# Last attention layer of a four-layer graph network on one Trainium2 core: probabilities with nodes on partitions, squares copied directly, and residual, input and result transfers issued from POOL

## Chip, core and metric

The kernel runs on one core of one Trainium2 chip. The time is the device time of one execution in microseconds (us), the median of three runs. In what follows PE is TensorE, DVE VectorE, ACT ScalarE, POOL GpSimd and SP SyncE; PEld is PE's loading of weights.

## What is computed

32 graphs of 512 nodes with 256 channels pass through four layers, all in float32 with one shared adjacency matrix `adj` of 512 x 512. Every layer has the form `x = x + L(relu(layernorm(x)))`. L0 is a two-step network with an unmasked and a masked graph attention, L1 a masked graph attention with one head, L2 an eight-head transformer block. The change touches L3, a graph attention with four heads of 64 channels:

```
q = (h @ W).reshape(B, N, 4, 64)
e = e_src[:, :, None, :] + e_dst[:, None, :, :]     # e_src, e_dst: q against the two halves of a
e = where(e >= 0, e, 0.2 * e)
e = where(adj > 0, e, -9e15)
out = elu(einsum('bijh,bjhd->bihd', softmax(e, axis=2), q))
```

So for each head a 512 x 512 matrix of probabilities is made from two vectors, and multiplied with 512 x 64 values. A node without neighbours gets the mean of all values.

## The kernel before

**Order.** The program is built as a list of operations of all 32 graphs, each with its engine, an estimated length, and what it reads and writes (`Graph.op`). `Plan.order` then places them like a list scheduler, at most six graphs in flight (`IN_FLIGHT`): of the operations that can start earliest the one with the earliest due time goes first. The due time comes from the graph's number times `PERIOD`, less the work behind the operation, plus a table of shifts by position (`SHIFTS`). Each engine then executes its instructions in this fixed order and waits for the others by semaphores. Buffers are taken in the same pass: `cell` (a part of 128 x 4 KB, 32 of them; a `Quad` is four in a row), `row`, `bank` (PSUM, 8), and in DRAM `page` and `sheet`.

**Transfers.** All are issued from SP (`transfer`): x is read twice per graph (`load`, L960), residuals are put away in DRAM pages and fetched again (`put_away` L967, `fetched` L973), the result is stored (L1588). L0 and L2 turn their layer input round by 32 x 32 squares: DVE transposes the squares (L636), then `crossed` writes them to a page (L615) and reads them back with the squares in place (L622). The eight heads of L2 do the same with their probabilities through a sheet (L1386 on DVE, L1391, L1399).

**Layer 3.** The input is transposed by PE (L655) and copied from PSUM by ACT (L663). The projection (L704) gives values and, for each head, three terms. `gat_probabilities` makes the probabilities already transposed, with the summed-over node on partitions. For each head PE spreads three vectors over all partitions by 4 transposes each (`rows_ps`, L720): the far term, a bias row, and the near term. DVE finds each row's masked maximum (L791, its output thrown away); POOL works the bias out of it (L806 to L809); ACT copies its row (L730); POOL adds the row to the transposed mask in two instructions (L821); DVE takes the maximum of two branches, which stands for the leaky relu, and adds it (L832, 4 per head); ACT takes the exponential (L840, 4 per head). POOL adds the probabilities up (L1484, L1488), a PE matmul with ones sums them (L1523), 16 matmuls give the output (L1502), and PE turns output and sums round (L1539). DVE scales by the reciprocal (L1548, L1551, L1561). Isolated nodes come apart from this: POOL and PE form the mean (`lonely`, L851, L852, L859), POOL spreads it (L870) and adds it (L1572).

Of the kernel before, what the change touches and what calls it, by code (L numbers as in the profile page):

```python
# [13 lines left out]
ALU = mybir.AluOpType  # L14
# [25 lines left out]
FLOOR = -(2.0**60)  # L40
TINY = 1e-30
# [3 lines left out]
CELL = NC * (C + 5)  # L45
ROW = N + 10
SMALL = 320
BUFFERS = {"cell": 32, "row": 7, "page": 48, "sheet": 12}
# [6 lines left out]
PERIOD = 50.7  # L55
# [3 lines left out]
    72, 50, 37, 26, 40, 30, 9, 57, 9, 9, 9, 9, 50, 27, -10, -39, 3, -6, 21, -19, -30, -122,  # L59
    -182, -23, -9, -33, 39, 5, -2, 1, -49, 1, 1, 0, -66, 1, 1, 1, 1, -16, 1, -38, -1, -71, -1,  # L60
    0, -23, 1, 2, -22, 1, 3, 1, -103, 1, 5, 1, -19, 1, 1, 19, 1, -26, 1, -3, 1, 1, 1, 14, 5, 0,
    1, 1, -10, 1, -2, 0, 0, 0, 1, 0, -1, 0, -1, 6, 0, -115, 19, 0, 7, -25, -6, 0, -32, -35, 0,
    68, 0, 35, 0, 93, -3, 2, 24, -51, 18, -11, 0, -7, 1, -75, 1, 1, 55, 0, 26, -26, 4, 3, 0,
    -39, -1, -162, -3, -56, -2, -13, 1, -20, -2, -37, -87, -26, -9, -7, -1, -27, -9, -52, -40,
    6, -52, -18, 0, -6, -4, 2, -5, -23, -88, 0, -14, -42, 12, -11, -1, -2, 6, -7, -10, -1, -49,
    -29, -3, -1, -23, 2, 0, -84, 10, -16, -46, -3, 7, 7, -17, 0, 0, 0, 0, -18, 0, 4, 144, 2, 0,
    -3, 0, -7, 2, -24, 27, -28, 31, -92, 47, -25, -10, 1, 0, -3, 0, 109, 0, -1, -75, -1, 0, 0,
    -3, 0, -7, -45, 0, 41, -1, 2, -7, 69, -15, -49, -3, -3, 0, 22, -97, -17, 4, -12, -9, 4, -53,
    -11, -1, -1, -5, 17, 5, 72, 47, 46, 74, 146, -16, -51, 41, -3, -13, -15, 2, 0, 1, 49, -18,
    -5, 30, 3, 4, 0, 0, -1, 0, 18, 14, -12, -32, 78, -1, 37, -82, -4, 7, -6, 0, 9, -3, -12, 9,  # L70
    0, -70, 20, 0, -10, 0, -1, 0, 23, 0, 0, -33, -10, 28, 83, 95, 37, 17, 76, -5, -36, -119,
    -25, -1, 92, 3, 0, 2, -3, 0, -24, 1, 0, -10, -5, -3, -36, -2, -46, -24, -68, 25, -10, -11,
    -13, -5, -2, -29, -22, -1, -1, -13, -2, 3, 14, 0, 0, 0, 28, 7, -83, -101, 7, 46, -9, -54,
    -46, 44, -24, 99, -5, -1, 0, 0, 75, 0, 0, 0, -10, 0, 1, 6, 0, 14, 0, 23, 13, -17, 53, 6, 87,
    -7, -16, 7, 3, 5, -1, -71, -87, 15, -12, 0, 11, 0, 0, 0, 8, 0, 0, -9, -8, 0, 23, 0, 0, -80,
    2, 0, 18, 0, 0, -3, 0, 0, 105, -13, -36, -11, -81, -30, -85, -143, -51, -24, -71, -29, -116,
    -48, -84, -82, -187, -154, -123, -175, -94, -43, -87, -62, 6, -91, -111, -160, -332, -388,
    -421, -351, -608, -395, -425, -396, -421, -341, -408, -335, -348, -464, -413, -372, -375,
    -378, -330, -297, -285, -312, -291, -315, -190, -199, -193, -90, -130, -236, -99, 76, -225,
    -189, -251, -299, -395, -387, -220, -242, -187, -183, -124, -28, -137, -109, -189, -108,  # L80
    -163, -117, -33, -55, -60, -125, -183, -244, -216, -176, -221, -264, -255, -199, -296, -271,
    -259, -434, -424, -521, -444, -340, -233, -214, -298, -180, -115, -52, -68, -145, -240,
    -205, -240, -241, -326, -236, -241, -474, -309, -46, -175, -128, -162, -177, -202, -326,
    -320, -212, -315, -229, -218, -238, -255, -252, -253, -294, -281, -196, -99, -190, 0, -59,
    -31, 0, -31, 3, -6, 2, 0, 2, -13, 0, 0, 0, 0, 16, 0, 141, -61, 0, 0, 0, -77, -2, -15, -29,
    -84, -35, -22, -60, -26, -26, -15, -26, -229, -39, -46, -103, -103, -16, -128, -41, -4, -61,
    -7, 35, -2, -9, 23, 3, 2, -22, -73, 5, -12, 2, 2, 2, -6, 2, 2, -5, 3, 2, 64, -18, 3, -11, 3,
    -24, 2, 2, 2, 3, 3, 42, 3, 1, 3, -26, 1, 3, -80, 17, -29, 27, -4, 3, 3, 3, 3, 3, 3, 3, -42,
    3, 0, -10, -36, -8, -69, -213, 23, -10, -20, 25, 26, 33, -18, 68, -12, -53, 17, 91, 94, 5,
    111, 25, 57, 164,  # L90
# [318 lines left out]
def adj_preln_kernel(  # L409
# [73 lines left out]
    self_biasT = const.tile([P, NC, N], BF, name="self_biasT")  # L483
    alone = const.tile([P, NC], FP, name="alone")
# [11 lines left out]
    l3_sb = weights(W_3, "l3_sb", TERMS * GAT_HEADS)  # L496
# [27 lines left out]
    ]  # L524
    smalls = [work.tile([P, SMALL], FP, name=f"smalls{k}") for k in range(IN_FLIGHT)]
# [15 lines left out]
    out_v = out.rearrange("b (c p) f -> b p c f", p=P)  # L541

    class Graph:
# [29 lines left out]
        def transfer(self, reads, writes, kbytes, emit, load=False):  # L573
            self.op("sp", 0.45, reads, writes, emit)
            self.op("dma", kbytes / RATE, reads, writes, lambda: None, 2.2 if load else 1.0)
# [200 lines left out]
        def gat_probabilities(self, holder, term, n, bias, biasT, own=False, after=()):  # L776
# [51 lines left out]
            for j in range(NC):  # L828
# [13 lines left out]
                    ),  # L842
                )
            return p, top

        def lonely(self, v, n):

            add = Buffer("row", 2, n)
# [116 lines left out]
        def put_away(self, src):  # L965
            page = Buffer("page", *src.shape)
            self.transfer([src], [page], 512, lambda: nc.sync.dma_start(page.ap, src.ap))  # L967
            return page
# [679 lines left out]
```

## Time and profile before

| | |
|---|---|
| median of 3 runs | 4420.88 us (4417.97 to 4422.98) |
| the profiled execution | 4422.42 us, span of its instructions 4420.6 us |
| mean granted PE clock | 0.979 |
| moved by DMA | 867.22 MB, 196 GB/s |
| busy: PE, DVE, POOL, ACT | 4170.8, 3662.7, 3034.1, 2924.3 us |

The span runs from the first instruction to the last. Busy time is the time in which an engine has at least one instruction, and a matmul's end is modelled, so that PE can be busy without being at its peak. The page cuts the span in 40 slices and gives busy tenths; it follows the chain of work that ended last; it lists groups of instructions by line with their count, busy time, mean duration and the idle time before them; and it lists DMA issues with their median time to landing. The trace answers the same questions for any stretch. Fp32 matmuls on full operands show as two instructions each.

### The profile page before, as it was taken

To read this page: it belongs to the slowest core of one execution; us is meant where nothing else is said; L and a number is where in the kernel's file an instruction comes from. 1 tells how busy PE (TensorE), PEld (TensorE's weight loads), DVE (VectorE), ACT (ScalarE), POOL (GpSimd) and SP (SyncE) were. 2 spreads that over 40 slices of the span, in tenths; PEclk is the share of its full clock that TensorE was granted. 3 is DMA by queue.
4 is the path that set the end of the run, shared out by engine and by line. 5 is a ranking of instruction groups with operands and counts; after the bars stand their busy time and mean duration, and the time that the engine had idled before them with its cause. 6 is when DMAs were issued, how large, how long until landed. Compare 5 with 4: busy or idle time off the path is not lost. (4 is left out here: it accounts for less than half of the span.)

```text
span 4420.6 us, 69315 instructions
## 1 busy us (share of the span) xinstructions
PE 4170.8 (94%) x21648; PEld 2583.3 (58%) x21648; DVE 3662.7 (83%) x9016; ACT 2924.3 (66%) x6309; POOL 3034.1 (69%) x3119
## 2 busy tenths in 40 slices
PE   6999999999999999999999999999999999999765
PEld 3656556665566666566666556666656666655332
DVE  3577888888888888888888888888889888888873
ACT  2556666777676667667667767666766766676653
POOL 1424766777776677776677777667777766777677
PEclk9999999999999999999999999999999999999877
DMA  3287667766767766766777667677667677766760
GB/s 121 84 226 218 187 190 220 218 202 181 215 199 211 224 200 201 204 204 194 222 215 204 201 200 211 194 224 210 205 205 206 192 217 219 201 200 186 231 175 29
DMA packets 441504, 867.22 MB, mean 196 GB/s; under 512 B 35248, under 2 KB 119728, under 8 KB 441136
## 3 DMA queue, kind: packets, MB, share of 16 engines
q1 hardware_dynamic: 439520, 862.78, 66.4%
q8 instruction: 173, 2.83, 0.3%
q14 instruction: 195, 1.60, 0.1%
q10 hardware_dynamic: 1616, 0.01, 0.0%
HBM read 443.23 MB, written 419.43 MB: 195 GB/s over the span
## 5 line engine op out<-in xcount | busy, mean ns | idle before, releaser
L1386 DVE STREAM_TRANSPOSE cells<-cells 128x512 f32<-128x512 f32 x1024 | 702.4, 698 | 148.8 <-ACT cells L1378 148.5
L1378 ACT ACTIVATE cells<-cells,smalls 128x512 f32<-128x512 f32 x1024 | 736.1, 719 | 114.0 <-DVE smalls L1367 105.8
L1367 DVE CUSTOM_DVE_ANT_0 cells<-bank,mask_bias 128x512 f32<-128x512 f32 x1024 | 686.9, 674 | 21.6 <-PE bank L1347 20.6
L821 POOL TENSOR_TENSOR cells<-mask_biasT,row 128x1024 f32<-128x1024 bf16 x320 | 682.3, 2155 | 16.2 <-ACT row L730 16.2
L791 DVE CUSTOM_DVE_ANT_0 masked<-bank,mask_bias 128x512 f32<-128x512 f32 x768 | 520.5, 678 | 71.1 <-PE bank L720 64.7
L683 PE MATMUL bank<-cells,mlp_sb 128*128 128x512 f32 x1024 | 473.1, 600 | 19.8 <-DMA cells<-page 13.2
L704 PE MATMUL bank<-fc_sb,cells 128*128 128x256 f32 (+1 forms) x2048 | 474.7, 381 | 1.5 <-DVE smalls L1367 0.8
L927 PE MATMUL bank<-cells 128*128 128x260 f32 x2048 | 465.1, 383 | 1.1 <-ACT cells L840 0.9
L603 ACT ACTIVATE cells<-cells,smalls 128x256 f32<-128x256 f32 x768 | 408.1, 592 | 74.7 <-POOL smalls L596 49.7
L1159 PE MATMUL bank<-cells 128*128 128x512 f32 x1024 | 450.9, 597 | 0.0
L927 PEld LDWEIGHTS bank<-cells 128*128 128x128 f32 x2048 | 387.9, 190 | 87.1 <-issue 24.9
L840 ACT ACTIVATE cells<-cells,smalls 128x512 f32<-128x512 f32 x512 | 348.5, 726 | 114.7 <-DVE cells L832 114.6
L704 PEld LDWEIGHTS bank<-fc_sb,cells 128*128 128x128 f32 x2048 | 376.9, 189 | 76.5 <-DVE cells L1442 19.0
L586 DVE BATCH_NORM_STATS2 smalls<-cells 128x6 f32<-128x256 f32 x768 | 311.3, 405 | 110.4 <-POOL cells L1222 101.3
L883 ACT ACTIVATE cells<-cells 128x512 f32<-128x512 f32 (+1 forms) x256 | 188.1, 735 | 292.9 <-DVE cells L946 111.3
L832 DVE SCALAR_TENSOR_TENSOR cells<-bank,smalls,cells 128x512 f32<-128x512 f32 x512 | 354.1, 740 | 30.5 <-POOL cells L821 27.0
L720 PEld LDWEIGHTS bank<-ident,smalls 128*128 128x128 f32 x2176 | 254.3, 141 | 212.6 <-issue 84.2
L720 PE MATMUL bank<-ident,smalls 128*128 128x128 f32 x2176 | 325.9, 284 | 54.2 <-POOL smalls L809 30.0
L1159 PEld LDWEIGHTS bank<-cells 128*128 128x128 f32 x1024 | 194.1, 193 | 230.2 <-issue 228.7
L1484 POOL TENSOR_TENSOR cells<-cells 128x1024 f32<-128x1024 f32 x128 | 302.3, 2372 | 19.2 <-PE bank L1502 8.4
L683 PEld LDWEIGHTS bank<-cells,mlp_sb 128*128 128x128 f32 x1024 | 186.0, 191 | 218.5 <-issue 170.3
L1347 PE MATMUL bank<-cells 32*128 32x512 f32 x2048 | 305.8, 644 | 5.7 <-DVE smalls L1367 4.8
(141 smaller groups left out, 8503.9 us busy)
## 6 DMA issues: line engine op xcount, KB each, us to landing
sheet<-cells SPq DMA_DIRECT2D x256, 1024.0 KB, 5.3
cells<-sheet SPq DMA_DIRECT2D x1024, 256.0 KB, 5.4
page<-cells SPq DMA_DIRECT2D x256, 512.0 KB, 3.4
cells<-page SPq DMA_DIRECT2D x192, 512.0 KB, 6.1
cells<-in_x_dram SPq DMA_DIRECT2D x64, 512.0 KB, 7.3
cells<-page SPq DMA_DIRECT2D x256, 128.0 KB, 2.9
out_dram<-cells SPq DMA_DIRECT2D x32, 512.0 KB, 5.4
mlp_sb<-in_L_gnn_mlp_w_dram SPq DMA_DIRECT2D x2, 512.0 KB, 6.7
```

The source lines that it names most:

```text
L603: lambda c=c: act.activation(xn[:, c, :], src[:, c, :], func, bias=off[:, c : c + 1], scale=rstd[:, c : c + 1],),
L683: lambda k=k, s=s, i=i, m=m, mm=mm: pe.matmul(mm.ap, w[:, k, cols + m * P : cols + (m + 1) * P], s.rows(i), start=(k == 0), stop=(k == nk ...
L704: pe.matmul(mm[:, :n], src[k // 2].nodes(k % 2, c), w[:, k, cols : cols + n], start=(k == 0), stop=(k == nk - 1),)
L720: pe.transpose(bc[:, c * P : (c + 1) * P], col(c).to_broadcast([P, P]), ident)
L791: lambda c=c: dve.tensor_tensor_reduce(masked, f2_ps.ap, bias[:, c, :], 1.0 - ALPHA, FLOOR, op0=ALU.add, op1=ALU.max, accum_out=top[:, c : ...
L821: lambda half=half: pool.tensor_add(p[half].ap, biasT[:, 2 * half : 2 * half + 2, :], w_row[:, None, :].to_broadcast([P, 2, N]),),
L832: lambda j=j, ph=ph, i=i: dve.scalar_tensor_tensor(ph[:, i, :], f1_ps.ap, term(2)[:, j : j + 1], ph[:, i, :], op0=ALU.max, op1=ALU.add,),
L927: pe.matmul(mm[:, :w1], p[j // 2][:, j % 2, c * P : (c + 1) * P], v[:, j, :], start=(j == 0), stop=(j == NC - 1),)
L1159: pe.matmul(mm.ap, h1[jh][:, i, m * P : (m + 1) * P], p[jh][:, i, :], start=(jh + i == 0), stop=(jh + i == 2),)
L1367: dve.tensor_tensor_reduce(tile(), sc[h].ap.rearrange("p (j f) -> p j f", j=NC), mask_bias[:, c, :].rearrange("p (j f) -> p j f", j=NC), - ...
L1378: lambda h=h, c=c, tile=tile: act.activation(tile(), tile(), AF.Exp, scale=-1.0, bias=low[:, c, h : h + 1], accum_out=sums[:, c, h : h + 1],),
L1386: dve.transpose(squared, squared)
```

## The change

Layer 3's probabilities are made with their own node on partitions. The input is turned round by `turned_round` instead of by PE. Per head one vector is spread by 4 PE transposes (`square_row`, its columns in the order of the squares), DVE adds mask and row and keeps both the sum and its maximum, POOL and ACT make the bias from the maximum, ACT applies Prelu with the near term as bias, then the exponential with its row sum accumulated, and DVE transposes the 32 x 32 squares. The squares of two heads are then copied from SBUF to SBUF by 16 transfers of 128 KB issued from SP (`squares_crossed`), each from 32 partitions to 32 partitions, and PE multiplies with the transposed result. The separate sums, the third term and the path for isolated nodes fall away in this layer (a row of equal masked values has equal probabilities). The nodes are then in square order, so the last residual is fetched in four quarters and the result stored in four quarters, and a mask in square order is made once at the start.

The pages' stores and loads, the second read of x and the first read of later graphs, the four quarters and the result are issued from POOL (`aside`); the transfers of `crossed`, the sheets, the direct squares and the loads at the start stay on SP. One `cell` more and three `row` fewer are held; `PERIOD` and all of `SHIFTS` are new. The diff, without `SHIFTS` and with small edits cut:

```diff
--- before
+++ after
-CELL = NC * (C + 5)
-ROW = N + 10
-SMALL = 320
-BUFFERS = {"cell": 32, "row": 7, "page": 48, "sheet": 12}
+CELL = NC * (C + 4)
+ROW = N + 8
+SMALL = 336
+BUFFERS = {"cell": 33, "row": 4, "page": 48, "sheet": 12}
...
-PERIOD = 50.7
+PERIOD = 53.2
...
-    self.op("dma", kbytes / RATE, reads, writes, lambda: None, 2.2 if load else 1.0)
+def transfer(self, reads, writes, kbytes, emit, load=False, issue=0.45, lag=2.2):
+    self.op("sp", issue, reads, writes, emit)
+    self.op("dma", kbytes / RATE, reads, writes, lambda: None, lag if load else 1.0)
+def aside(self, reads, writes, kbytes, emit, load=False):
+    self.op("pool", 1.2, reads, writes, emit)
+    self.op("dma", kbytes / RATE, reads, writes, lambda: None, 2.8 if load else 1.6)
...
+def square_row(self, holder, col, dst):
+    bc = Buffer("bank", N)
+    def emit():
+        for c in range(NC):
+            pe.transpose(
+                bc.ap.rearrange("p (q c i) -> p q c i", q=NC, i=SQUARE)[:, :, c, :],
+                col(c).to_broadcast([P, P]),
+                ident,
+            )
+    self.op("pe", 0.47, holder, [bc, *dst], emit)
+    return bc
+def masked_probabilities(self, holder, far, near, n, table, p, tile, parts, sums=None):
+    bias, key = table
+    f2_ps = self.square_row(holder, far, [p])
+    top = self.small(f"top{n}", NC)
+    m = self.small(f"m{n}", NC)
+    for c in range(NC):
+        self.op(
+            "dve", 0.77, [f2_ps, [(key, c, q) for q in range(P // SQUARE)]], [top, parts(c)],
+            lambda c=c: dve.tensor_tensor_reduce(
+                tile(c),
+                f2_ps.ap.rearrange("p (a i) -> p a i", i=tile(c).shape[2]),
+                bias[:, c, :].rearrange("p (a i) -> p a i", i=tile(c).shape[2]),
+                1.0, LOWEST,
+                op0=ALU.add, op1=ALU.max, accum_out=top[:, c : c + 1],
+            ),
+        )
+    self.op(
+        "pool", 0.35, [top, *holder], [top],
+        lambda: pool.tensor_add(top.ap, top.ap, near()),
+    )
+    def emit():
+        act.activation(m.ap, top.ap, AF.Prelu, alpha=ALPHA)
+        act.activation(m.ap, m.ap, AF.Copy, scale=-1.0)
+    self.op("act", 0.45, [top], [m], emit)
+    for c in range(NC):
+        self.op(
+            "act", 0.72, [*holder, parts(c)], [parts(c)],
+            lambda c=c: act.activation(
+                tile(c), tile(c), AF.Prelu, bias=near()[:, c : c + 1], alpha=ALPHA
+            ),
+        )
+    for c in range(NC):
+        def emit(c=c):
+            out = {} if sums is None else {"accum_out": sums[0](c)}
+            act.activation(tile(c), tile(c), AF.Exp, bias=m[:, c : c + 1], **out)
+        self.op(
+            "act", 0.72 if sums is None else 0.82, [m, parts(c)],
+            [parts(c), *([sums[1]] if sums else [])], emit,
+        )
+        def emit(c=c):
+            squared = tile(c).rearrange("p a (l i) -> p a l i", i=SQUARE)
+            dve.transpose(squared, squared)
+        self.op("dve", 0.69, [parts(c)], [parts(c)], emit)
+def squares_crossed(self, src, dst, read, write, kbytes):
+    squares = P // SQUARE
+    for turn in range(squares):
+        for l in range(squares):
+            to = (l + turn) % squares
+            def emit(l=l, to=to):
+                nc.sync.dma_start(
+                    dst(slice(to * SQUARE, (to + 1) * SQUARE), l),
+                    src(slice(l * SQUARE, (l + 1) * SQUARE), to),
+                )
+            self.transfer([read], write(l, to), kbytes, emit, True, 0.6, 1.5)
...
 def load(self, dst, src, writes, kbytes, name, after=()):
-    self.transfer(
-        [after] if after else [], writes, kbytes,
-        lambda: nc.sync.dma_start(dst(), src), True,
-    )
+    if name in LOADS or not after:
+        self.transfer(
+            [after] if after else [], writes, kbytes,
+            lambda: nc.sync.dma_start(dst(), src), True,
+        )
+    else:
+        self.aside(
+            [after], writes, kbytes, lambda: pool.dma_start(dst(), src), True
+        )
     if name in LOADS:
         plan.ops[-2].due = plan.ops[-1].due = LOADS.index(name) - 1e6
 def put_away(self, src):
     page = Buffer("page", *src.shape)
-    self.transfer([src], [page], 512, lambda: nc.sync.dma_start(page.ap, src.ap))
+    self.aside([src], [page], 512, lambda: pool.dma_start(page.ap, src.ap))
     return page
 def fetched(self, page, after):
     dst = Buffer("cell", *page.shape)
-    self.transfer(
-        [page, *after], [dst], 512, lambda: nc.sync.dma_start(dst.ap, page.ap), True
-    )
+    self.aside(
+        [page, *after], [dst], 512, lambda: pool.dma_start(dst.ap, page.ap), True
+    )
+    return dst
+def fetched_squares(self, page, after):
+    dst = Buffer("cell", *page.shape)
+    for q in range(P // SQUARE):
+        def emit(q=q):
+            pool.dma_start(
+                dst[q * SQUARE : (q + 1) * SQUARE],
+                page[:, q, :].rearrange("(c i) f -> i c f", i=SQUARE),
+            )
+        self.aside([page, *after], [[(dst, "from", q)]], 128, emit, True)
...
+    quarters = range(P // SQUARE)
+    page = [("mask page", 0)]
+    self.transfer(
+        [[("mask", c) for c in range(NC)]], [page], 256,
+        lambda: nc.sync.dma_start(mask_page, mask_bias),
+    )
+    for q in quarters:
+        def emit(q=q):
+            nc.sync.dma_start(
+                mask_square[q * SQUARE : (q + 1) * SQUARE],
...
-    xt = self.fetched(self.x_page, after)
+def add_to_xt(self, y, after, squares=False):
+    xt = (self.fetched_squares if squares else self.fetched)(self.x_page, after)
+    landed = [(xt, "from", q) for q in range(P // SQUARE)]
...
 def layer3(self):
     xn = self.normalized(self.xt, AF.Relu, 1)
-    hT = self.transposed(xn)
-    q = Buffer("cell", NC, C)
-    f = self.small("f16", NC, TERMS, GAT_HEADS)
-    n = C + TERMS * GAT_HEADS
+    hT = self.turned_round(xn)
+    v = Buffer("cell", NC, C)
+    f = self.small("f8", NC, PAIR, GAT_HEADS)
+    n = C + PAIR * GAT_HEADS
...
-    mean = self.lonely(q, C)
-    after = []
-    sums, rows = [], []
+            act.activation(v[:, c, :], mm[:, :C], AF.Copy)
+        self.op("act", 0.57, [mm], [f, v.part(c)], emit)
+    sums = self.small("sumh", NC, GAT_HEADS)
+    rinv = self.small("rinvh", NC, GAT_HEADS)
+    z = Buffer("cell", NC, C)
     for g in range(GAT_HEADS // 2):
-        ps = []
-        total = Buffer("cell", 2, N)
+        p = Quad(NC, 2, NC, P)
+        pT = Quad(NC, 2, NC, P)
         for i in range(2):
             h = 2 * g + i
-            p, top = self.gat_probabilities(
-                [f], lambda t, h=h: f[:, :, t, h], h % 2, mask_bias, mask_biasT, False,
-                after,
+            self.masked_probabilities(
...
-            ps.append(p)
-            halves = Buffer("cell", 2, N)
-            self.op(
-                "pool", 2.4, p, [halves],
-                lambda p=p, halves=halves: pool.tensor_add(halves.ap, p[0].ap, p[1].ap),
-            )
-            self.op(
-                "pool", 1.27, [halves], [total.part(i)],
-                lambda i=i, halves=halves, total=total: pool.tensor_add(
-                    total[:, i, :], halves[:, 0, :], halves[:, 1, :]
-                ),
-            )
-        sums.append(total)
+        self.squares_crossed(
+            lambda at, to, p=p: p[at, to].rearrange("p h c i -> p (h c i)"),
+            lambda at, l, pT=pT: pT[at, l].rearrange("p h c i -> p (h c i)"),
+            [(p, i, c) for i in range(2) for c in range(NC)],
+            lambda l, to, pT=pT: [[(pT, l, to)]],
+            128,
+        )
         acc = Buffer("bank", N)
         r = Buffer("row", N)
...
+        def emit(g=g, pT=pT, acc=acc):
+            for j in range(NC):
+                for i in range(2):
+                    d = (2 * g + i) * GAT_DIM
+                    pe.matmul(
+                        acc[i * GAT_DIM : (i + 1) * GAT_DIM, :],
+                        v[:, j, d : d + GAT_DIM],
+                        pT[:, :, i, :, j * SQUARE : (j + 1) * SQUARE].rearrange(
+                            "p l c i -> p c l i"
+                        ),
+                        start=(j == 0),
+                        stop=(j == NC - 1),
+                    )
+        squares = [(pT, l, to) for l in range(NC) for to in range(P // SQUARE)]
+        self.op("pe", 3.5, [v, squares], [acc, r], emit)
...
-    def emit(acc=acc):
-        for h in range(GAT_HEADS):
-            d = slice(h * 32, (h + 1) * 32)
-            pe.matmul(
-                acc[d, :], ones[:, d], sums[h // 2][:, h % 2, :], start=True, stop=True
-            )
...
+        self.op("pe", 0.5, [r, z], [back], emit)
         def emit(g=g, back=back):
+            hs = slice(2 * g, 2 * g + 2)
+            dve.reciprocal(rinv[:, :, hs], sums[:, :, hs])
...
-    self.elu_to_xt(z, [rows[1]])
+        self.op("dve", 0.9, [back, sums], [rinv, z], emit)
+    self.elu_to_xt(z, [z.part(0)], True)
...
-    self.transfer([res], [], 512, lambda: nc.sync.dma_start(out_v[i], res.ap))
-    plan.writers["left", i] = [plan.ops[-1]]
+    rows_v = out[i].rearrange("(q c i) f -> q i c f", q=NC, i=SQUARE)
+    stores = []
+    for q in range(P // SQUARE):
+        self.aside(
+            [res], [], 128,
+            lambda q=q: pool.dma_start(
+                rows_v[q], res[q * SQUARE : (q + 1) * SQUARE]
+            ),
+        )
+        stores += plan.ops[-2:]
+    plan.writers["left", i] = stores
```

## The prediction

> **What bounds the kernel now.** I read three views in this order. First the page's head and its slices:
>
> ```profile
> span 4420.6 us, 69315 instructions
> ...
> PE 4170.8 (94%) x21648; PEld 2583.3 (58%) x21648; DVE 3662.7 (83%) x9016; ACT 2924.3 (66%) x6309; POOL 3034.1 (69%) x3119
> ...
> PE   6999999999999999999999999999999999999765
> ...
> PEclk9999999999999999999999999999999999999877
> DMA  3287667766767766766777667677667677766760
> ```
>
> TensorE is full from the second slice to the 37th; only the last 160 us thin out. Next the chain of waits, by time: the same work returns at a fixed distance.
>
> ```profile
> 3066.39 7.03 PE bank L927 x32
> ...
> 3195.52 7.03 PE bank L927 x32
> ...
> 3325.22 7.03 PE bank L927 x32
> ```
>
> One graph leaves every 129.7 us, so a time saved per graph counts 31 times; the other 400 us are the first graph's way in and the last one's way out. Then the busy time of each engine in a stretch of ten periods (columns: stretch, length, busy of PE, PEld, DVE, ACT, POOL, then granted clock, DMA share, GB/s), and that of single lines in it, here the spreading transposes L720, the layer-3 matmuls L1502, and POOL's L821:
>
> ```profile
> 1000.00:2297.00 1297.00, 1274.74 (x6697) 794.75 (x6696) 1132.66 (x2774) 906.10 (x1967) 943.38 (x963) 1.00 0.70 205
> 1000.00:2297.00 1297.00, 123.72 (x838) 96.38 (x836) 1.00 0.70 205
> 1000.00:2297.00 1297.00, 77.48 (x320) 19.41 (x320) 1.00 0.70 205
> 1000.00:2297.00 1297.00, 255.36 (x120) 1.00 0.70 205
> ```
>
> Per period: PE 127.5 of 129.7 us (idle 2.2), DVE 113.3, ACT 90.6, POOL 94.3, DMA 0.70 x 129.7 = 90.8 at full clock. PE bounds; DVE has 16.4 us of slack. What PE's 2.2 us waits for, in the same stretch, is mainly DVE:
>
> ```profile
> PE bank L1523 <- DVE cells L1297: 11.5, 10, 1.2
> PE bank L720 <- DVE smalls L1149: 6.0, 9, 2.7
> ```
>
> **PE, per graph.** All durations are a line's busy time in the ten periods divided by its count. Removed: 32 of the 84 spreading transposes of L720 (three rows per head become one), 32 x 0.1476 = 4.72 us; the 8 transposes of layer 3's input (L655, 34.82/240 = 0.145), 1.16; the mean row for isolated nodes (2 of L859, 0.3185 each), 0.64; the matmuls that sum the probabilities (L1523, 10.66/10), 1.07; the 4 transposes that turn the sums round (L1539, 0.15), 0.60. Sum 8.19 us. The 32 attention matmuls stay; they now read their moving operand in runs of 32 elements. L1412 reads so already: 7.54 us for 32 rounds of 256 columns, 0.236 a round, against 0.484 for 512 in L1502: no dearer, so 0. PE's work becomes 119.3 us.
>
> **DVE.** Removed: 16 combinations L832 at 0.693 = 11.1, and the sums' L1548 and L1551, 0.4. Added: 16 square transposes at L1386's 0.686 = 11.0, two 512-wide ones for the layer's input (L636, 0.67) = 1.3, two reciprocals 0.4; the 16 masked maxima now keep their output (0.682 as L1367, not 0.675) 0.1. Net +1.3: 114.6 us. **ACT.** 16 Prelu passes at the exponential's 0.685 = 11.0, the accumulators on 16 exponentials (0.811 as L1378, less 0.685) 2.0, eight small ones 1.7; out go two evictions L663, four rows L730, the mean and sums rows, 4.5. Net +10.2: 100.8 us, with one table load in the built instruction list as before. Neither sets the end by itself; both lose cover.
>
> **POOL.** Removed: 8 adds L821 at 2.13 = 17.0, the sums L1484 and L1488, 9.4 + 5.5, four heads' small steps 4.2, lonely and spread 3.9, L1572 3.0. With four small adds back, 52.1 us remain. Added are 21 DMA issues: 6 stores of 512 KB to pages, 5 such loads, 4 quarter loads, 4 quarter results, 2 reads of x. No transfer is issued from POOL in this trace. SP issues the same page store (L967) in 0.34 us, the lower end; a POOL pass over a tile of that size (L1245) takes 2.37, the upper end. A multi-step POOL instruction on 4 columns (L595) takes 1.04; I take 1.1, nearest to it: 23 us, between 7 and 50. The waits move too: SP stood 28.3 us per period before these lines (L967, L973, L960, L1588), where nobody minded; on POOL the layer-norm steps, the head's small add and the residual adds are queued behind, and ACT and DVE wait for those. So POOL takes 52 + 23 + 0 to 28 = 75 to 103 us, and covers it if the issue is cheap.
>
> [...]
>
> **DMA and SP.** Added: 32 direct copies of 128 KB, from 32 partitions to 32 others, and one turned input (512 KB out, 4 x 128 KB back): 5.24 MB on 26.7 MB. At the present price (90.8 us for 26.7 MB) that is 17.8 us: 108.6 of DMA time. No copy from SBUF to SBUF is in the trace. The nearest rows:
>
> ```profile
> cells<-sheet SPq DMA_DIRECT2D x1024, 256.0 KB, 5.4
> ...
> cells<-page SPq DMA_DIRECT2D x256, 128.0 KB, 2.9
> ```
>
> Without the page's write between, a square could cost half as much per KB (saves 7 us); if each used the engines alone for the whole 2.9 us, 32 would take 93 us, the far end. I take the average price, nearest to the first row, whose destination is also 32 partitions. SP issues 65 transfers per graph now, 87 after; at 0.43 us (L1399) to 0.53 (L1391) about 38 us, which its waits hide.
>
> [...]
>
> **The sum.** If PE kept its 2.2 us of idle, a period would be 121.5. But DVE then has 6.9 us of slack where it had 16.4, and PE's waits are for DVE. I let the idle grow as the slack shrinks (2.2 x 16.4 = 36; idle x with x(x + 119.3 - 114.6) = 36 gives 4.1; this rule is my choice): period 123.4. 31 x 6.3 = 195 us. The way in is nearly untouched. The new shifts, the 33rd cell and the three rows fewer change only the order; in the built list POOL's and SP's instructions repeat graph by graph, so I charge nothing for them beyond the idle, and A and C stand for a better and a worse order. At the end, POOL's L821, L1484 and L1488 hold 23.7% of the chain's last 221 us, some 52 us; in their place come 16 rows of ACT at 0.72 + 0.72 + 0.20 = 26 us, the last pair's 16 issues and landing (7 + 5) and the turned input's two trips (3.4 + 2.9), and three more result transfers: 5 us less, from 15 less to 10 more. 4420.6 - 195 - 5 = 4220. The profiled execution took 4422.4 (span 4420.6) and the median is 4420.88, so the same number stands for the median.
>
> **Rivals.** (A) The idle does not grow, because the new order of work was fitted to the new loads: 4420.6 - 31 x 8.2 = 4166, range 4140 to 4190. For it: PE's waits now are short, 1 to 3 us. 20%. (B) My forecast, 4190 to 4280, 45%. (C) The freed PE waits for the longer way: squares must be issued and land (12 us a pair) where probabilities were used in place, and eight cells are held meanwhile. Spread over six graphs in flight that is 2 us a period, 4282; with ACT and DMA crowded as well, up to 4411. 15%. (D) Nothing measurable, 4412 to 4430 (0.2% is about what a measurement can tell here): 3%. It would need the two losses to meet the gain by chance. (E) Slower, by the DMA engines at the squares: the price k of a KB against the average decides. DMA time is 94.4 + 14.3k; at a share of 0.95 the period passes 129.7 from k = 2.0, and at 2.25 it is 133, or 4530. For it: a short queue of 32-partition pieces; against: stretches of 10 us already move up to 312 GB/s, and 259 are needed. 9%. (F) Slower, by POOL: with all 28 us of waits, POOL fills a period of 129.7 from 2.3 us an issue; at 2.6 it is 135, 4585. 8%.
>
> Range 4150 to 4430: it leaves out a part of A and most of E and F. Faster 20 + 45 + 15 = 80%, same 3%, slower 17%.
>
> **What would show it.** In ten middle periods of the changed kernel: PE busy about 119 a period and the period 123; DVE at 93%; DMA share near 0.88 at 259 GB/s; POOL about 60% busy outside its issues. PE's waits should name DVE. Wrong if PE is under 93% with DMA releasing it (C, E) or with POOL (F), or if a square lands later than 5 us, or an issue on POOL takes over 2 us.

## The result, and the profile after

The changed kernel takes 5179.98 us (median of 4 runs, 5177.31 to 5184.72) where the kernel before takes 4421.93 (4 runs beside it): ratio 1.1716, 95% interval 1.1696 to 1.1737. It is 758 us slower; 4220 was forecast.

The page of the kernel after: head, slices, two lines that wait long, one of DVE and one of PE (busy, mean ns | idle before the line and what ended it), and three DMA rows (median us to landing).

```profile
span 5179.0 us, 68292 instructions
...
PE 4261.1 (82%) x19920; PEld 2557.7 (49%) x19920; DVE 3592.4 (69%) x9078; ACT 3222.4 (62%) x7333; POOL 2136.7 (41%) x2731
...
PE   6988888888888888888888888888888888888643
...
PEclk9999999999999999999999899999899999998866
DMA  3366777777777777777777777777777777777873
...
L1505 DVE STREAM_TRANSPOSE cells<-cells 128x512 f32<-128x512 f32 x1024 | 681.1, 691 | 754.8 <-DMA sheet<-cells 739.9
...
L1615 PE MATMUL bank<-cells 128*64 128x512 f32 x1024 | 307.4, 755 | 265.6 <-DMA cells<-cells 239.6
...
cells<-sheet SPq DMA_DIRECT2D x1024, 256.0 KB, 7.2
cells<-cells SPq DMA_DIRECT2D x1024, 128.0 KB, 4.2
page<-cells POOLq DMA_DIRECT2D x192, 512.0 KB, 5.8
```

PE is at 80 to 89% in nearly every slice where it was at 90 or more, from the third slice on: the loss is in every graph, not at an end. No other engine has become full. And a line that the change did not touch, L1505 (L1386 before), stands 754.8 us; its count is as it was, and so, within 1%, is its mean. It transposes the squares of the eight-head layer's probabilities. Before, it stood 148.8 us, and for ACT:

```profile
L1386 DVE STREAM_TRANSPOSE cells<-cells 128x512 f32<-128x512 f32 x1024 | 702.4, 698 | 148.8 <-ACT cells L1378 148.5
```

The waits of the kernel after (total us, times, longest) name what it stands for:

```profile
DVE cells L1505 <- DMA sheet<-cells: 739.9, 95, 11.3
ACT cells L1497 <- DVE smalls L1486: 687.7, 427, 9.7
...
PE bank L1615 <- DMA cells<-cells: 239.6, 38, 27.9
```

DVE waits 95 times, some 8 us each, for a store of the sheet; in the kernel before no DVE wait for such a store is found. ACT then waits for DVE. PE's own largest wait, for the squares of layer 3, is a third as large. One such wait, on DVE's timeline (start, us, [idle before it and its releaser]) and on SP's:

```profile
2405.51 0.08 DVE L1486 DVE_READ_ACCUMULATOR2_ANT smalls<- 128x1 f32 x1
2415.67 0.71 DVE L1505 STREAM_TRANSPOSE cells<-cells 128x512 f32<-128x512 f32 x1 [10.07 <-DMA sheet<-cells]
2416.31 0.38 DVE L593 BATCH_NORM_STATS2 smalls<-cells 128x6 f32<-128x256 f32 x1
```

```profile
2394.60 13.81 SPq L928 DMA_DIRECT2D cells<-cells  x16
2408.52 13.16 SPq L1510 DMA_DIRECT2D sheet<-cells  x2
```

DVE finishes at 2405.6 and stands 10 us. The store that it waits for is issued by SP only at 2408.52, because SP was issuing 16 squares of layer 3 until 2408.41; it lands 7.1 us later. In those 10 us everything behind the transpose on DVE, the layer norms of other graphs too, stands as well. The second store of the pair can't go before DVE has gone on: hence 13.16 us for two issues.

**What the wait is.** Two blocks of 128 nodes share one buffer of four cells, row `j` of block `c` at element `1024*j + 512*c`. The store of block 0 reads rows that the transposes of block 1 never touch. In the built instruction list of the changed kernel, 184 of the 1024 transposes nevertheless wait for a transfer, some of them for two: 156 waits are for the store of the other block, 111 for reads of a sheet. In the list of the kernel before not one does, though these lines of code are the same. What differs is the tile that holds all cells: 32 x 1044 = 33408 elements to a partition before, 33 x 1040 = 34320 after. I built both with the tile made a little wider and nothing else changed: 34368 instead of 34320 elements gives 0 such waits, 34432 gives 0, 34328 and 34384 leave 184; the kernel before with 33424 gets 242, with 33412 33, with 33472 none. All four widths that are a multiple of 64 elements have none, all five others some. So the dependency tracking tells the interleaved rows of two blocks apart only at some widths of the tile, and the 33rd cell together with the smaller cell lost that. These widened builds weren't run on the chip; what was run is the layout that makes the two blocks lie one after the other, which also leaves 0.

**Per graph.** In 1000 to 3500 us of each trace: the graphs in it are the matmuls there over those of one graph (676.5 before, 622.5 after). The row for the kernel after (stretch, length, busy PE, PEld, DVE, ACT, POOL, clock, DMA share, GB/s):

```profile
1000.00:3500.00 2500.00, 2136.08 (x10076) 1287.22 (x10075) 1803.12 (x4548) 1631.17 (x3720) 1085.87 (x1385) 0.93 0.75 208
```

10076 / 622.5 = 16.2 graphs: a period of 154.5 us, PE busy 132.0 and idle 22.5 of it. The clock in the trace's records falls to one half in spells of 3.41, 6.83 or 10.24 us: 361.8 us of this stretch, of which PE is busy for 266.9. Of all of L1615's matmuls in the trace 38% start in a spell and take 1.01 us on average, the others 0.60. Half of the 361.8 us, taken as lost, is 11.2 us a graph: an estimate from the recorded clock, at its upper end, since PE is not busy throughout. The same for all kernels that matter below (us a graph; the columns of work and loss rest on that estimate):

| kernel | period | PE work at full clock | lost at half clock | PE idle |
|---|---|---|---|---|
| before | 130.5 | 127.9 | 0.4 | 2.2 |
| after | 154.5 | 120.8 | 11.2 | 22.5 |
| blocks apart | 140.0 | 122.3 | 4.8 | 12.9 |
| and squares unread | 135.8 | 123.1 | 3.1 | 9.6 |
| and no squares | 134.0 | 122.6 | 3.2 | 8.2 |
| forecast | 123.4 | 119.3 | 0 | 4.1 |

### The profile page after: what moved, and what is told of

It reads as the page before. It is cut to its first block, busy times and chain, and to the rows that moved or that the text cites. A ratio compares the mean times of both kernels' runs of the same rounds, so it can differ in the third digit from the quotient of the medians.

```text
span 5179.0 us, 68292 instructions
## 1 busy us (share of the span) xinstructions
PE 4261.1 (82%) x19920; PEld 2557.7 (49%) x19920; DVE 3592.4 (69%) x9078; ACT 3222.4 (62%) x7333; POOL 2136.7 (41%) x2731
## 5 line engine op out<-in xcount | busy, mean ns | idle before, releaser
L1505 DVE STREAM_TRANSPOSE cells<-cells 128x512 f32<-128x512 f32 x1024 | 681.1, 691 | 754.8 <-DMA sheet<-cells 739.9
L1497 ACT ACTIVATE cells<-cells,smalls 128x512 f32<-128x512 f32 x1024 | 733.1, 717 | 692.3 <-DVE smalls L1486 687.7
L1615 PE MATMUL bank<-cells 128*64 128x512 f32 x1024 | 307.4, 755 | 265.6 <-DMA cells<-cells 239.6
L899 ACT ACTIVATE cells<-cells,smalls 128x512 f32<-128x512 f32 x512 | 353.1, 713 | 268.7 <-DVE smalls L877 266.7
L1016 PEld LDWEIGHTS bank<-cells 128*128 128x128 f32 x2048 | 380.4, 191 | 129.6 <-issue 37.0
L711 PE MATMUL bank<-l_sb,cells 128*128 128x264 f32 (+1 forms) x1024 | 309.0, 451 | 153.8 <-DVE smalls L747 109.7
L1531 PE MATMUL bank<-cells 128*32 128x256 f32 x4096 | 289.1, 430 | 101.0 <-DMA cells<-sheet 50.9
L907 ACT ACTIVATE cells<-cells,smalls 128x512 f32<-128x512 f32 x512 | 362.8, 709 | 0.1
L916 DVE STREAM_TRANSPOSE cells<-cells 128x512 f32<-128x512 f32 x512 | 339.1, 689 | 32.7 <-ACT cells L907 32.2
L1466 PE MATMUL bank<-cells 32*128 32x512 f32 x2048 | 357.8, 644 | 2.3 <-DVE smalls L1486 2.2
L877 DVE CUSTOM_DVE_ANT_0 cells<-bank,mask_square 128x512 f32<-128x512 f32 x512 | 334.5, 671 | 6.5 <-PE bank L859 5.5
L1249 POOL TENSOR_TENSOR cells<-cells 128x512 f32<-128x512 f32 x64 | 81.2, 1268 | 618.9 <-DVE cells L776 618.8
L711 PEld LDWEIGHTS bank<-l_sb,cells 128*128 128x128 f32 x1024 | 218.2, 225 | 226.0 <-issue 177.1
```

The costliest lines, as they stand in the source:

```text
L711: pe.matmul(mm[:, :n], src[k // 2].nodes(k % 2, c), w[:, k, cols : cols + n], start=(k == 0), stop=(k == nk - 1),)
L899: lambda c=c: act.activation(tile(c), tile(c), AF.Prelu, bias=near()[:, c : c + 1], alpha=ALPHA),
L907: act.activation(tile(c), tile(c), AF.Exp, bias=m[:, c : c + 1], **out)
L916: dve.transpose(squared, squared)
L1016: pe.matmul(mm[:, :w1], p[j // 2][:, j % 2, c * P : (c + 1) * P], v[:, j, :], start=(j == 0), stop=(j == NC - 1),)
L1466: pe.matmul(sc[h].ap, qT[d, g, c * P : (c + 1) * P], kT[d, g, :], start=True, stop=True,)
```

## The experiments

The theories: **H**, the false wait for the stores; **C** and **E**, the squares of layer 3, by the longer way or by the DMA engines; **F**, the issues on POOL; **O**, the order of the work. The quoted expectations carry more letters, each explained there. Where one of them takes it that the kernel before has the false wait too, only covered, it is wrong: its list has none.

### The two blocks one after the other (e1), and the same before (e2)

```diff
-                p = Quad(NC, 2, PACK, P)
+                p = Quad(2, NC, PACK, P)
-                            return p[:, :, c % 2, h, :]
+                            return p[:, c % 2, :, h, :]
-                            p[:, :, c % 2].rearrange("p j h f -> p j (h f)"),
+                            p[:, c % 2].rearrange("p j h f -> p j (h f)"),
```

> The changed kernel with one edit: in the eight-head layer the two node blocks of a probability buffer lie one after the other instead of interleaved row by row (same order of work on every engine, same transfers). Theory H (the interleaved halves): DVE's square transposes of a second block stand waiting for the first block's store, 25 us of the 155.4 us period, because the store's rows and the transposes' rows interleave in one buffer and the new order puts the two blocks close together. Then the waits of this line go and the period falls by up to 25 us, to 130 to 135, so 4400 to 4560 us. Rival Q (SP is late: the direct squares hold its queue and the eight-head stores behind it): the wait only moves to the next reader of the squares, and the time stays over 5000. Rival P (the transfers on POOL): no change, 5180.

> Control: the kernel before with the same edit of the eight-head buffer. In its trace the square transposes never wait for a store. Theory H: nothing to remove, 4420 within 0.3%. If it gets faster by over 1%, the layout costs something else (a bank or port effect of the stride) and H is not the whole story.

Measured: e1 4744.65 us (1.0731, 1.0708 to 1.0753), e2 4423.32 (1.0000, 0.9991 to 1.0010). The lines of e1 that answer to those above:

```profile
L1505 DVE STREAM_TRANSPOSE cells<-cells 128x512 f32<-128x512 f32 x1024 | 677.8, 690 | 29.1 <-ACT cells L1497 28.9
L1615 PE MATMUL bank<-cells 128*64 128x512 f32 x1024 | 302.8, 745 | 260.0 <-DMA cells<-cells 221.9 <-DVE cells L1040 12.6 <-DMA sheet<-cells 11.0
```

The transposes' idle falls from 754.8 to 29.1 us and none of it is for a store; 435 of the 758 us are back. It stays above the 4400 to 4560 that H gave, because the squares and what follows below remain. The edit by itself is worth nothing, as e2 shows. H is shown for 57% of the loss, and the squares' wait is untouched by it.

### The issues on POOL: undone after (e3), added before (e4), undone on e1 (f1)

```diff
-            self.aside([src], [page], 512, lambda: pool.dma_start(page.ap, src.ap))
+            self.aside([src], [page], 512, lambda: nc.sync.dma_start(page.ap, src.ap))
...
```

e3 and f1 do so at all five places, e4 the reverse in the kernel before; the planned order stays.

> The changed kernel with its 21 POOL-issued transfers per graph issued from SP at the same places of the planned order. Theory H: POOL's issues (0.56 to 0.79 us each, 13 us a period of a POOL that is 42% busy) are not the cause, so 5100 to 5300, no gain. Rival P: the time falls below 4800. Rival Q: SP, with 21 issues more per graph, gets later still, over 5300.

> The kernel before with the same kinds of transfer (page stores and loads, x, result; 15 to 16 per graph) issued from POOL, its planned order unchanged. Theory H: POOL is 73% busy there, 16 issues at 0.6 us add 10 us to 94 of 130 and some waits for POOL, so between 4410 and 4560. Rival P: 4700 or more, since this part alone would carry the loss.

> The kernel with the blocks apart (4745 us, period 139.9), and its 21 POOL-issued transfers per graph issued from SP at the same places of the order. Theory P (the move to POOL costs by itself, since POOL's compute stands behind transfers that wait): the kernel before lost 151 us by it and the changed kernel got back 80, so 4590 to 4690. Rival Q (SP late with the direct squares): SP gets 21 issues more and PE waits longer for the squares, 4745 or more.

Measured: e3 5099.75 (1.1532, 1.1513 to 1.1551), 80 us less than after; e4 4572.93 (1.0344, 1.0327 to 1.0361), 151 more than before; f1 4723.90 (1.0693, 1.0677 to 1.0709), 21 less than e1. Each lies between or just beside the ranges of its theories, so the issues cost something, but with the false wait gone only 21 us of what is left, and in e4 the order had been planned for SP. F as a bound is out: POOL is 41% busy.

### The squares: left out (f2), copied but not read (g2), on two queues (f3); the sheet (f4)

```diff
# f2
-                        nc.sync.dma_start(
-                            dst(slice(to * SQUARE, (to + 1) * SQUARE), l),
-                            src(slice(l * SQUARE, (l + 1) * SQUARE), to),
-                        )
+                        pass
# f2 and g2
-                def emit(g=g, pT=pT, acc=acc):
+                def emit(g=g, pT=p, acc=acc):
# f3
-                        nc.sync.dma_start(
+                        (nc.scalar if l % 2 else nc.sync).dma_start(
# f4
-                sheet = Buffer("sheet", NC, 2, PACK * P)
+                sheet = Buffer("sheet", 2, NC, PACK * P)
```

All stand on e1. f2 and g2 sum layer 3 over wrong pairs of nodes.

> The kernel with the blocks apart, without the 32 direct copies of layer 3: its attention matmuls read the untransferred buffer (this leaves out that the squares change places, so layer 3's sums are over wrong pairs; counts, shapes and order of all other work are the same). Theory Q: PE idles 6.4 us a period before these matmuls, its DVE follower waits behind it, and the eight-head stores stand behind the copies on SP, so 10 us or more a period go: under 4450. If only PE's own wait goes: 4545. Rival P or an order that is bad elsewhere: 4650 or more.

> The kernel with the blocks apart; all 32 direct copies run, but layer 3's matmuls read the buffer before the copies (this leaves out that the squares change places, so its sums are over wrong pairs). Without the copies it took 4527, with copies and readers 4745. If the copies cost by the wait for them (PE's fixed order stands behind), 4520 to 4590. If they cost by crowding, on SP or on the 16 DMA engines, whoever reads them: 4680 to 4745.

> The kernel with the blocks apart, every second direct copy issued from ACT, at the same place of the order. Theory Q in its narrow form (16 issues of 0.63 us one after the other make the squares late, 10 us a pair): 5 us a pair are saved on SP, PE's 6.4 us a period shrink, 4600 to 4690, with 16 issues added to an ACT that is 71% busy. If landing or crowding is the matter, not the issue: within 0.5% of 4745. If the issues hold up ACT's own chain: slower than 4745.

> The kernel with the blocks apart, and the two blocks apart in the DRAM sheet too, so that a block's reads do not stand behind the other block's store and a store writes runs of 8 KB. PE idles 3.5 us a period before the eight-head matmuls for these reads. Theory S (the same interleaving in the sheet): those go, 4640 to 4700. Otherwise within 0.5% of 4745.

Measured: f2 4527.06 (1.0246, 1.0231 to 1.0261); g2 4595.07 (1.0390, 1.0375 to 1.0406); f3 4756.50 (1.0762, 1.0746 to 1.0778); f4 4722.14 (1.0681, 1.0655 to 1.0707). Where g2's PE stands at the two sums over transferred data, heads (L1531) and layer 3 (L1615); ahead of them the line of the heads in e1:

```profile
L1531 PE MATMUL bank<-cells 128*32 128x256 f32 x4096 | 286.1, 426 | 142.6 <-DMA cells<-sheet 93.4 <-issue 28.1 <-DMA cells<-cells 10.1
```

```profile
L1531 PE MATMUL bank<-cells 128*32 128x256 f32 x4096 | 299.2, 441 | 214.2 <-DMA cells<-sheet 106.2 <-issue 32.6 <-DMA page<-cells 30.7
L1615 PE MATMUL bank<-cells 128*64 128x512 f32 x1024 | 251.0, 628 | 43.8 <-DVE cells L916 19.9 <-DVE cells L1040 18.7 <-DMA cells<-sheet 3.9
```

With nothing to wait for at L1615 its idle falls from 260.0 to 43.8 us, and its mean from 745 to 628 ns because fewer of these matmuls start in a spell of half clock: 34% in e1, 7% in g2, with a mean of 1.0 us there and 0.60 us outside in both. Of the squares' 218 us (e1 to f2), 150 go when nothing reads the copies (the wait and what stands behind it; 4595 is 5 us over the range given for that) and 68 when they do not run. Issuing them from two queues doesn't help (12 us more, within the spread of the runs), nor does a sheet in two parts help much (22 us less): neither the issue nor the sheet's layout sets it. And in g2 PE stands longer than in e1 before the sum of the heads, half of it for the reads of the sheet, an unchanged transfer. In f2 these reads are PE's largest wait (112.9 us).

### The planner's landing times, with the fitted order (g1, g3), and telling it of the false wait (g4)

```diff
# g1 (on e1), g3 (on f4 with f1's edit)
-    def transfer(self, reads, writes, kbytes, emit, load=False, issue=0.45, lag=2.2):
+    def transfer(self, reads, writes, kbytes, emit, load=False, issue=0.45, lag=4.2):
...
# g4 (on the kernel after)
-                    reads = [qT.part(g), kT.part(g), before]
+                    reads = [qT.part(g), kT.part(g), before, [(sheet, 0)] if c > c0 else []]
```

> The kernel with the blocks apart (4745 us), whose planner is told that transfers land later (loads by 2.0 us, stores by 1.0, direct copies by 1.8, so a direct copy 4.3 us after its issue as measured); the buffers and all work stay, only the order changes. Theory O (what is left is an order that counts on transfers landing earlier than they do: PE idles 11 us a period before the squares, the sheet reads and the layer-3 input): those idles shrink, 4500 to 4650. Otherwise, if the engines or the DMA set the rest, 4720 or more; the shifts were fitted to the other times, so somewhat slower would not count against O by itself.

> All that helped together: blocks apart in the buffer and in the sheet, all transfers issued from SP, planner told of later landings. Theory O: 4450 to 4620. To beat the kernel before it must be under 4410, which I give one chance in ten.

> The changed kernel as it was (blocks interleaved in the buffer), but the planner is told that a second block's scores follow the first block's store, so that it puts the two further apart; no work is changed. Theory H (hidden wait, met because the planner does not know of it): the 25 us a period before the square transposes go mostly, 4650 to 4850. If the wait is not a matter of order, 5050 or more.

Measured: g1 5228.58 (1.1831, 1.1811 to 1.1851), g3 5185.66 (1.1734, 1.1710 to 1.1758), g4 5528.41 (1.2496, 1.2467 to 1.2524). All far worse, and they tell nothing about landing times: `SHIFTS` holds a correction for each operation of one exact plan, and an edit of the plan sets them against other neighbours. (With the table emptied, g1's landing times give 4723 us, i1 below.) In g4 the wait itself nearly goes: L1505 stands 164.8 us, 18.5 of them for a store, and the time is worse all the same. The question needed plans without the table.

### Without the table of shifts (h1 to h4)

`SHIFTS = ()` in the kernel before (h1), in e1 (h2), in the kernel after (h3) and in f2 (h4).

> The kernel before with its table of shifts emptied, nothing else: the planner places the work by due times from chain lengths alone. Theory O (an order that fits the chip is worth much, and the one before fits better than the one after): well above 4422, between 4700 and 5200 us, with PE's idle at 10 us a period or more. Rival W (the changed work itself costs what is missing, the order little): under 4550 us.

> The changed kernel with the eight-head input's blocks one after the other, table of shifts emptied. Its plan gives each period 8 us less of TensorE. Theory O: it rises less than the kernel before did and stands within 3% of that one's time without shifts, or below. Rival W: it stands 7% or more above that one, as it does with the shifts (4745 against 4422).

> The changed kernel as it is (blocks interleaved), table of shifts emptied. If the store's wait at the square transposes comes with any order of this work: 8% to 10% above the same kernel with the blocks apart and no shifts, and the transposes' idle before them about 25 us a period. If only the fitted order puts the two blocks' stores back to back: within 2% of it.

> Blocks apart, table of shifts emptied, and the squares' 32 copies left out, so that layer 3's sums are over wrong pairs. If the squares cost what they cost in the fitted order: 218 us below the version with them. Theory O says in addition that this one stands below the kernel before without shifts, by up to the 8 us a period (250 us) of TensorE's work that is gone; rival W says that it stands 2% above, as with the shifts.

Measured: h1 4687.45 (1.0604, 1.0586 to 1.0622), h2 4917.68 (1.1120, 1.1098 to 1.1142), h3 5254.59 (1.1884, 1.1857 to 1.1911), h4 4812.41 (1.0878, 1.0849 to 1.0908). The transposes in h1, then in h3:

```profile
L1353 DVE STREAM_TRANSPOSE cells<-cells 128x512 f32<-128x512 f32 x1024 | 699.9, 697 | 136.5 <-ACT cells L1345 136.3
```

```profile
L1472 DVE STREAM_TRANSPOSE cells<-cells 128x512 f32<-128x512 f32 x1024 | 684.0, 691 | 594.6 <-DMA sheet<-cells 550.9 <-ACT cells L1464 35.2 <-ACT cells L1352 7.9
```

The false wait costs without the table too (h3 to h2: 337 us, 6.9%, between the two expectations), and in the kernel before it comes in none of the three orders traced. h2 stands 4.9% above h1, between what O (within 3%) and W (7%) expected; h4, without squares, still 2.7% above, near what W said. So the fit of the table explains a part at most: an order made by the same rule leaves the gain missing. The squares' price hangs on the order, however: h2 to h4 it is 105 us, where 218 had been expected.

### Truer landing times, without the table (i1, i2)

```diff
-    def transfer(self, reads, writes, kbytes, emit, load=False, issue=0.45, lag=2.2):
+    def transfer(self, reads, writes, kbytes, emit, load=False, issue=0.45, lag=4.2):
-        self.op("dma", kbytes / RATE, reads, writes, lambda: None, lag if load else 1.0)
+        self.op("dma", kbytes / RATE, reads, writes, lambda: None, lag if load else 2.0)
...
```

In i1 also 3.3 us for a square (1.5) and 4.8 and 2.6 for POOL's transfers (2.8 and 1.6). i1 stands on h2, i2 on h1.

> Blocks apart, table of shifts emptied, and the planner's landing times made longer, about as the traces show them (reads 2.2 to 4.2 us behind the transfer, stores 1.0 to 2.0, squares 1.5 to 3.3, POOL's 2.8 and 1.6 to 4.8 and 2.6). Theory S (misplaced sums: the plan believed in early landings): under 4800 us, against 4918 with the old landing times, and PE's idle before the sums over sheet reads and squares falls to less than half. Theory L (the longer way itself: graphs stay longer, buffers and graphs in flight run out, so truer times only move the wait elsewhere): 4850 to 5000 us.

> The kernel before, table of shifts emptied, the same longer landing times (reads 2.2 to 4.2, stores 1.0 to 2.0). Theory S: nothing to mend here, its reads had 12.8 us of cover, 4687 give or take 1%. Theory L: its graphs pass fewer transfers in a row, so at most the same small change, within 2% of 4687.

Measured: i1 4723.40 (1.0692, 1.0676 to 1.0708), 194 less than h2; i2 4710.36 (1.0660, 1.0643 to 1.0678), 23 more than h1. PE at the two sums, in h2 and then in i1:

```profile
L1498 PE MATMUL bank<-cells 128*32 128x256 f32 x4096 | 311.5, 456 | 240.5 <-DMA cells<-sheet 173.4 <-issue 26.1 <-DMA cells<-page 11.5
...
L1582 PE MATMUL bank<-cells 128*64 128x512 f32 x1024 | 297.1, 733 | 202.9 <-DMA cells<-cells 174.1 <-DVE smalls L1453 8.7 <-DMA cells<-sheet 8.5
```

```profile
L1498 PE MATMUL bank<-cells 128*32 128x256 f32 x4096 | 279.3, 419 | 93.1 <-DMA cells<-sheet 48.9 <-DMA cells<-page 12.0 <-DVE smalls L1453 9.1
...
L1582 PE MATMUL bank<-cells 128*64 128x512 f32 x1024 | 257.8, 649 | 122.4 <-DMA cells<-cells 85.6 <-ACT cells L577 22.0 <-DVE smalls L1453 8.5
```

The waits for transfers of sheet and squares go from 347.5 us (173.4 + 174.1) to 134.5. Theory S holds for that part: the plan of the changed kernel puts these sums right behind where it believes the data lands (2.4 us behind, median, for the sheet's reads, 0.6 for the squares; 7.9 for the sheet's reads in the plan of before), and the reads land 1 to 2 us later than they did before (7.2 us to landing, 6.8 in e1, 5.4 before). The later landing is not the changed work's: in h1 and i2, the kernel before with an emptied table, the reads take 6.8 us as well. There it costs little, since h1's plan puts the sum 10.5 us (median) behind them: PE stands 19.2 us for them. Under equal conditions, no table and truer times, i1 and i2 are 0.3% apart, inside their intervals: the change with its false wait removed is neither gain nor loss there. No kernel tried beats the one before.

## Why the prediction was wrong

**The failed step** is the sentence that the new shifts, the 33rd cell and the three rows fewer change only the order, so that nothing was charged beyond the idle. The cell's new size and number changed what the transposes wait for: 435 of 758 us, on a line that the forecast had no reason to price, because the code of it is the same. It could have been seen beforehand in the built instruction list, by counting waits for transfers on each line, and I read that list for counts and order alone. No rival had it.

**The squares**, rival C, 2 us a graph: right in kind, too small in size. They cost 218 us in the fitted order, 7.0 a graph, 150 of them through their readers (105 us in all without the table). E is refuted: a square lands in 4.2 us, under the 5 that I had set, and the DMA share is 0.75 after, 0.81 in e1. Their DMA time, from the shares of g2 and f2, is 0.84 x 135.8 - 0.73 x 134.0 = 16 us a graph against 14.3.

"SP ... about 38 us, **which its waits hide**": SP's time may be hidden, its order is not. Sixteen squares in a row held the store in the timeline above for the first 3 of DVE's 10 us.

**PE's work** went, by the table, from 127.9 to between 120.8 and 123.1 us a graph, 4.8 to 7.1 less where 8.2 was forecast; which lines hold the difference is not shown. (The table's row before is 130.5 us where the forecast has a period of 129.7: the chain's three rows are 129.1 and 129.7 apart, and its ten periods hold 9.9 graphs by the count of matmuls, so a graph was taken some 1% too short.) **The idle** of 4.1 became 8.2 even without squares or false wait: I let it grow with DVE's shrinking slack, but it is the reads of the sheet that PE then stands for most (112.9 us before L1528 in f2, 3.5 a graph). **The half clock** had no term at all and takes 3.2 us a graph even there, by the same estimate. Work 3.3, clock 3.2 and idle 4.1 make the 10.6 us by which f2's period of 134.0 exceeds 123.4. So the terms of the 960 us between 4220 and 5180 are: false wait 435, squares 218, and 307 for these three, which were read from the trace and not taken away one by one.

**The sign.** PE under 93% with DMA releasing it was to speak for C or E, and it came: PE is at 85% in the middle, its largest wait the squares' 239.6 us. By itself it would have led to the smaller term. The larger one shows as a wait of DVE (739.9 us at L1505), and PE stands behind DVE and POOL (229 and 235 us of its waits in the whole trace).

**What was right**: DVE 114.6 us a graph forecast, 1803.12 / 16.2 = 111 measured; ACT 100.8, measured 101; POOL's issues were put at 1.1 us and take 0.55 to 0.79 by line (medians; the dearest is x), 12.5 us a graph, so POOL is at 67. The longest issue on POOL took 0.86 us, far from F's price of 2.3.

**What stays open**: why the reads of the unchanged sheet land later in every order but the fitted one of the kernel before. Neither the squares nor POOL's transfers are needed for it (7.0 us without squares in f2, 6.8 with all issued from SP in f1, and 5.3 in the fitted order with transfers on POOL, e4). Also open: how much of POOL's 151 us in e4 is the plan's ignorance of it; whether a tile of 34368 elements alone brings the kernel after to e1's time, which the lists suggest and no run shows; and what a table of shifts fitted to truer landing times would give.

## What to carry to other kernels

Before pricing a change of buffers, count in the built instruction list, line by line, the waits for transfers, before and after: here a line with the same code got 184 waiting transposes of 1024 when the tile changed its size, and the 95 waits that the trace shows for a store, 7.8 us long on average, kept DVE standing 739.9 us. The two blocks, one written while the other is stored, did better one after the other in the buffer than interleaved, by 435 us (e1). The hand-fitted order was worth 266 us here, and only for its own plan: an edit is compared best with the table emptied on both sides, and with the landing times in the plan as the trace has them.

## What the runs showed of the hardware that was not expected

PE's idle came with a second loss here. The granted clock falls to half in spells whose lengths are 3.41 us and its multiples, 4 of them in 1000 to 3500 us before, 57 after, 31 in e1, 19 in f2 (mean granted clock of the stretch 1.00, 0.93, 0.97 and 0.98). PE was idle for 57% to 100% of the 3.41 us ahead of each of them in the kernel after and in e1 (for 41% at the least in before, f2, g2, h1 and i1). In e1, the 34 waits of over 3 us before L1615 are followed by matmuls of 1.06 us (75th percentile of that line there; its median is 0.59). In the kernel after the spells cost 11.2 us a graph by the table's estimate, half as much as the idle itself.
